# A Fourier layer on one core: norms applied at the images, mixing on two engines, half blocks of y, and pools that stay open

## The chip, the cores and the metric

The kernel runs on one core of a Trainium2 chip. The metric is the device time of one execution in microseconds (us). The time before is the median of three executions. The profile comes from one more execution with the hardware profiler; its clock starts at the start of the profiled span, and all positions below are on that clock. TensorE (PE) does matmuls, VectorE (DVE), ScalarE (ACT) and GpSimd (POOL) work elementwise, and SyncE (SP) only issues DMA transfers. ACT and POOL issue transfers too.

## The reference, cut to what matters

The program is two layers on an image x of 256 x 256 pixels and 128 channels. Layer 0 is an attention along rows with a gate; it ends near 1660 us in the profile and nothing of it changes. Layer 1 regards its input as 256 tokens of 128 x 128 pixels (two halves of 128 tokens, one row of the partitions for each token), attends between tokens in Fourier space, and then runs a block on groups of four tokens. Only this last block is touched:

```python
attn = instance_norm(attn + tokens, ...)         # y in the kernel
h0 = instance_norm(attn, norm2_w, norm2_b)
h1 = fno_layer(h0, mix_wr[0], ..., norm=True, act=True)
h2 = fno_layer(h1, mix_wr[1], ..., norm=True)
out = instance_norm(h2, mon_w, mon_b) + attn

def fno_layer(x, ...):
    skip = einsum('bihw,oi->bohw', x, sw) + sb    # a 4x4 mix of the tokens of a group
    xf = spectral_conv(x, wr, wi, bias)           # 32 x 16 Fourier modes, each a 4x4 complex mix
    if norm: xf = instance_norm(xf)               # mean 0 and variance 1 of each image
    y = xf + skip
    return gelu(y) if act else y
```

The result is added to x. The norm of the spectral part is one factor for each token, called rs: the inverse root of its energy over the modes. So rs times the synthesised image plus the skip product may as well be computed as rs times (image plus skip over rs), if what follows can scale.

## The kernel before, in words

**Tiles.** A half has 128 tokens and 16384 pixels. It is walked in 16 blocks of NB = 2048 pixels, or 32 half blocks of HB = 1024 (512 KB in f32). `by_turn` splits a block into four groups of image columns (j), which belong to the four turned copies that the inverse transform over the height makes from 32 rows of modes each. Half 0's images stay in memory (`blocks`); half 1's y goes to DRAM (`yd`) and comes back.

**Steps of the block.**
- `y_blocks(a, ...)` makes y. For half 1 it writes it with POOL's queue (L1338).
- `first_modes(a)` loads the modes of y, normalises them, mixes them with the 4x4 weights (`mix_modes`), and transforms them over one axis into `Gd1` in DRAM (`synth_modes`, L566 to L589: matmuls, copies out of PSUM by ACT and DVE, writes issued by POOL and ACT).
- `first_images(a)` makes h1 of each block: `skip` (32x32 pieces, L1211) plus `image` (inverse transform of the modes loaded by `load_modes`, L1200), then GELU on ACT (L1499). In the same loop PE transposes the block before and transforms it forward into `Yd`. For half 0 it also computes w = lam y + x on ACT and POOL, and writes it to `wd`.
- `second_modes(a)` reads `Yd` back as YT, finishes the forward transform (L1568), mixes (`mix_modes`), and synthesises into `Gd2`. It also gathers the factors kap and c0 of the last norm.
- `output(a, b)` makes a block of h2 by `skip` and `image`, scales on ACT (L1621), adds w on DVE and writes it out by POOL (L1628). `output_0` runs it for half 0. `Output1` runs it for half 1, and makes w from y and x there (L1674), five half blocks of it ahead.

**Mixing** (`mix_modes`) is 16 products of 128x512 on DVE (L1358), each then added up in PSUM by a matmul with the identity (L1367). After it come the squares on ACT (two, 128x512), the energy by 16 small matmuls (L1376), `rsqrt` (small DVE and ACT operations, L35 to L43), a matmul that spreads the factor over all partitions (L1390), its copy (L1396) and the scaling of both accumulators into Z (L1399). Only then can synthesis begin.

**Order.** The compute engines and SP run in the order in which the program emits work, since the whole block stands under a manual schedule. Stages are generators; the order is made by hand by calling `next` on two of them in turn, at the end of the file. Each engine takes its instructions in order, so a waiting instruction holds all behind it on that engine, SP's loads included.

The stages on the profile's clock are:
- 2047 to 2196: `first_modes(0)` woven with 24 half blocks of `y_blocks(1)`
- 2196 to 2336: `first_images(0)`
- 2336 to 2387: the last 8 half blocks of y and the start of `second_modes(0)`
- 2387 to 2478: `second_modes(0)` and `first_modes(1)`. Both mix, one product each in turn, and then synthesise.
- 2478 to 2680: `first_images(1)` and `output_0` in turn. The pools are changed at the start: `xp` closes with yctx, and `op0` and `hp1` open.
- 2680 to 2755: `second_modes(1)`, with `Output1.ahead` beside its end
- 2755 to 2896: `Output1.run`

The pools are regions of SBUF. A new pool may lie where an old one was, and then its first use waits for the last use of the old. The buffers with names (`xt` 3, `yt` 2, `gs` 3) are taken in turn within a pool, and each waits for the last reader of what it held.

Of the kernel before, what the change touches and what calls it, by code (L numbers as in the profile page):

```python
# [512 lines left out]
def layer1(tc, I, C, ident, x1d, upool, U, stats2, mv2, out):  # L513
# [9 lines left out]
    with ExitStack() as ctx:  # L523
# [681 lines left out]
        def skip(ps, src, blk, stop):  # L1205


            for j in range(4):
                for i in range(4):
                    r, o = slice(32 * i, 32 * i + 32), slice(32 * (i ^ j), 32 * (i ^ j) + 32)  # L1210
                    nc.tensor.matmul(rows_of(ps[j][o, :]), blk[r, r], src[r, j], start=True, stop=stop)  # L1211
# [78 lines left out]
        for a in range(2):  # L1290
            h = Half()
            halves.append(h)
            h.col = sp.tile([P, 16], FP, name=f"col_{a}")
            h.bl0 = sp.tile([P, P], FP, name=f"bl0_{a}")
            h.Gd1 = dram.tile([32, 4, 64, P], FP, name=f"Gd1_{a}")
            h.Gd2 = dram.tile([32, 4, 64, P], FP, name=f"Gd2_{a}")
            h.Yd = dram.tile([H, 32, P], FP, name=f"Yd_{a}")
# [43 lines left out]
        def mix_modes(wp, mk, psum, F, l, tag, out, constant=()):  # L1341
# [3 lines left out]
            T, G = P, P // 4  # L1345
            acc = [psum.tile(f"{tag}acc_{r}") for r in range(2)]
            by_c = [z.rearrange("p (c t) -> p c t", c=4) for z in acc]
# [5 lines left out]
            def product(k):  # L1353
                i, x, r, dst = steps[k]
                t = mk("m", [P, 4, G, 4], f"{tag}m_{k}")
                f = F[:, :, x, :].rearrange("p c (g i) -> p c g i", i=4)[:, :, :, i]
                w = mixw[r][:, :, 16 * l + 4 * i : 16 * l + 4 * i + 4]
                nc.vector.tensor_tensor(t, bc(f, 3, 4), bc(w, 2, G), ALU.mult)  # L1358
                return t.rearrange("p c g o -> p (c g o)")

            t = product(0)
            for k, (i, x, r, dst) in enumerate(steps):
                now = t
                if k < 15:
                    t = product(k + 1)
                yield 0.6
                nc.tensor.matmul(acc[dst], ident, now, start=(i == 0 and x == 0), stop=(i == 3 and x == 1))  # L1367
            sq = mk("f", [P, 2, 4, T], tag + "sq")
            for r in range(2):
                nc.scalar.activation(sq[:, r], by_c[r], AF.Square)  # L1370
            yield 1.8

            en = psum.tile(tag + "ens")
            for c in range(4):
                for r in range(2):
                    nc.tensor.matmul(  # L1376
                        en[:, 0:1], sq[:, r, c, :], om0[:, min(c, 1) : min(c, 1) + 1],
                        start=(c == 0 and r == 0), stop=(c == 3 and r == 1),
                    )
            yield 0.9  # L1380
            rs = wp.tile([P, 2], FP, tag=tag + "rs", name=tag + "rs", bufs=1)
            rsqrt(nc, wp, rs[:, 0:1], en[:, 0:1], EPS, "rq")
            left = rs[:, 1:2]
            nc.vector.tensor_mul(left, rs[:, 0:1], rs[:, 0:1])
            nc.vector.tensor_mul(left, left, en[:, 0:1])
            dg = mk("m", [P, P], tag + "dg")
            nc.vector.tensor_scalar(dg, ident, rs[:, 0:1], None, ALU.mult)
            yield 1.8
            ps = psum.tile(tag + "rsp")
            nc.tensor.matmul(ps[:, 0:T], ones, dg, start=True, stop=True)  # L1390
            for k, (x, m) in enumerate(constant):
                nc.tensor.matmul(
                    ps[0:1, 256 : 256 + T], x, m, start=(k == 0), stop=(k == len(constant) - 1)
                )
            rsb = mk("m", [P, T], tag + "rsb")
            nc.scalar.copy(rsb, ps[:, 0:T])  # L1396
            Z = mk("f", [P, 4, 2, T], tag + "Z")
            for r in range(2):
                nc.vector.tensor_tensor(Z[:, :, r, :], by_c[r], bc(rsb, 1, 4), ALU.mult)  # L1399
            if constant:  # L1400
                nc.vector.tensor_copy(Z[0:1, 0, 0, :], ps[0:1, 256 : 256 + T])
            else:
                nc.vector.memset(Z[0:1, 0, 0, :], 0.0)
            nc.vector.tensor_scalar(Z[0:32, 0], Z[0:32, 0], wsyn[0:32, 0:1], None, ALU.mult)
            out[:] = [Z, left]
            yield 1.8

        def first_modes(a, wp, mk, psum, gts):
# [34 lines left out]
            z = []  # L1443

            yield from mix_modes(wp, mk, psum, F, 0, f"x{a}", z, ((sig, blk[0]), (ch[:, 2:3], ident)))
            Z = z[0]
            for c in range(4):
                synth_modes(wp, psum.pool, Z, P, h.Gd1, f"g1{a}", turned=True, chunk=c, ptag=psum.tag, gts=gts,
                            queues=(nc.gpsimd, nc.scalar))
                yield 2.7  # L1450

        def first_images(a, wp, yp, psk, pst, first=None):
# [5 lines left out]
            def load(b):  # L1458
                if a == 1:
                    ys[b] = yp.tile([P, NB], FP, tag="xt", name=f"y2_{b}")  # L1460
                    nc.sync.dma_start(ys[b], ydv[:, a, b * NB : (b + 1) * NB])
# [27 lines left out]
            for b in range(17):  # L1489
# [4 lines left out]
                if b < 16:  # L1494
                    ps = [psk.tile(f"ups_{a}_{b}_{j}") for j in range(4)]
                    skip(ps, by_turn(ys.pop(b) if a else hb[b]), h.bl0, False)
                    image(ps, gss.pop(b), bs4)
                    for j in range(4):
                        nc.scalar.activation(by_turn(hb[b])[:, j], rows_of(ps[j]), AF.Gelu)  # L1499
# [40 lines left out]
        def second_modes(a, wp, mk, psum, gts, yts):  # L1540
# [6 lines left out]
            def load(c):  # L1547
                yp, tag, bufs = yts[c]
                YT[c] = yp.tile([P, 2, 2, 512], FP, tag=tag, name=f"YT_{a}_{c}", bufs=bufs)
                for hc in range(2):  # L1550
# [7 lines left out]
            load(0)  # L1558
            yield 6.0
            if a:  # L1560
                load(1)
            for c in range(4):
# [12 lines left out]
                for k in ((2,), (3,), (), ())[c] if a else ((1,), (2, 3), (), ())[c]:  # L1575
                    load(k)
                if c < 3:
                    yield 4.0
            yield None
            z = []  # L1580
            yield from mix_modes(wp, mk, psum, F, 1, f"z{a}", z)
            Z, left = z
            Fw = mk("m", [P, 2, P], f"Fw_{a}")
            nc.vector.tensor_scalar(Fw, F[:, 0], hw0, None, ALU.mult)
            for c in range(4):
                if c == 2:

                    ps = psum.tile(f"cvps_{a}")
                    for i in range(4):
                        for r in range(2):  # L1590
                            nc.tensor.matmul(
                                ps[:, 0:P], F[:, i, r, :] if i else Fw[:, r, :], Z[:, i, r, :],
# [4 lines left out]
                    nc.vector.bn_aggr(h.col[:, 10:12], hstat.rearrange("p k s -> p (k s)"))  # L1597
                synth_modes(wp, psum.pool, Z, P, h.Gd2, f"g2{a}", chunk=c, ptag=psum.tag, gts=gts,
                            queues=(nc.gpsimd, nc.scalar))
                yield 2.7  # L1600
# [3 lines left out]
            nc.vector.scalar_tensor_tensor(hv, ps[:, 0:1], 4.0, hv, ALU.mult, ALU.add)  # L1604
            nc.vector.tensor_add(hv, hv, left)
            rsqrt(nc, wp, kap, hv, EPS, "rq")
            nc.vector.tensor_mul(kap, kap, ch[:, 4:5])
            nc.vector.tensor_mul(c0, hm, kap)
# [5 lines left out]
        def output(a, b, gs, w, psk):  # L1614

            kap, c0 = (halves[a].col[:, k : k + 1] for k in (8, 9))
            ps = [psk.tile(f"h2ps_{a}_{b}_{j}") for j in range(4)]
            skip(ps, by_turn(hb[b]), blk[1], False)
            image(ps, gs, bs4)
            for j in range(4):  # L1620
                nc.scalar.activation(  # L1621
                    by_turn(hb[b])[:, j], rows_of(ps[j]), AF.Identity, bias=c0, scale=kap
                )
# [6 lines left out]
        def output_0(pools, psk):  # L1630
# [3 lines left out]
            def load(b):  # L1634
                wp, gp, bufs, _ = pools
                t = wp.tile([P, NB], FP, tag="xt", name=f"w_{b}", bufs=bufs)
                nc.sync.dma_start(t, wd[:, b * NB : (b + 1) * NB])
                gs = gp.tile([P, 4, P], FP, tag="gs", name=f"gs3_0_{b}", bufs=3 if gp is xp else 2)
# [5 lines left out]
            for b in range(16):  # L1644
                if b not in got:
                    load(b)
                if b < 15 and pools[3]:
                    load(b + 1)
                t, gs = got.pop(b)
                yield from output(0, b, gs, [t[:, 0:HB], t[:, HB:]], psk)  # L1650
                yield

        class Output1:
# [23 lines left out]
            def ahead(self):  # L1677
                self.more = self.wp
                self.load(0)
                self.load(1)  # L1680
                yield 1.0
                for k in range(5):
                    self.add(k)
                    if k < 3:
                        self.load(k + 2)
                    yield 1.0

            def run(self, psk, more):
# [11 lines left out]
                for k in (5, 6, 7):  # L1700
# [14 lines left out]
        with tc.manual_schedule(engines=COMPUTE | {ENG.SP}):  # L1715
# [8 lines left out]
            with yctx:  # L1724
# [7 lines left out]
                with tc.tile_pool(name="mp1", bufs=1) as wp:  # L1732
# [10 lines left out]
                    for _ in range(3):  # L1743
                        next(m1)
                    run(iter(lambda: next(m0), None))
                    for _ in m0:
                        next(m1)
                    pools = [xp, xp, 3, True]
                    o0 = output_0(pools, bq)
# [7 lines left out]
                    pools[3] = False  # L1757
                    for _ in range(3):
                        next(o0)
            with tc.tile_pool(name="op0", bufs=4) as op, tc.tile_pool(name="hp1", bufs=2) as wp:  # L1760
                pools[:] = [op, wp, 4, True]
                due, begun = 0.0, False
                for done in first_images(1, wp, op, bq, br, (y2, g2)):
                    if not done:
                        due += 0.9
                        begun = due > 0
                    if begun:
                        next(o0, None)
                    if done and begun:
                        due -= 1.0  # L1770
                run(o0)
            pz.release_now()
            with tc.tile_pool(name="op1", bufs=2) as op:
# [179 lines left out]
```

## Time and profile before

| what | us |
|---|---|
| time, median of 3 | 2890.99 (2890.81 to 2894.68) |
| profiled execution | 2898.24 |
| its span | 2896.1 |
| PE busy | 2640.4 (91%) |
| DVE busy | 2007.2 (69%) |
| POOL busy | 1647.4 (57%) |
| ACT busy | 1463.0 (51%) |

The mean granted clock of PE is 0.948 of full speed. Most of the busy time is layer 0's; the changed part is the last 849 us, so shares of the whole span tell little about it. The rows that matter to it, with their count and mean of one:

| line | operation | count | mean ns |
|---|---|---|---|
| L1358 | DVE product 128x512 | 64 | 684 to 691 |
| L1367 | PE matmul with the identity, 128x512, two passes a product | 128 | 592 |
| L1399 | DVE scaling of Z, 128x512 | 8 | 682 to 686 |
| L1334 | DVE y out of PSUM, 128x256 | 256 | 415 |
| L1499 | ACT GELU 128x512 | 128 | 601 |
| L1621 | ACT scale and bias 128x512 | 128 | 777 |
| L1674 | DVE w = lam y + x, 128x1024 | 32 | 1285 |
| L303 | POOL tensor_tensor 128x512 (layer 0) | 512 | 1270 |
| L327 | POOL tensor_tensor 128x256 (layer 0) | 256 | 732 |
| L299 | POOL tensor_tensor 128x1024 (layer 0) | 256 | 2370 |

The busy time of PE is modelled from pipelined matmuls, and one pass of L1367 follows the next after 0.43 us. DVE's products in a row follow each other after 0.61 us, and those of L1334 after 0.35. The first product of `skip` in each block of `first_images(1)` (tile `ups`) starts at 2487.77, 2511.27, 2523.45, 2532.87, 2544.99 and so on to 2665.68 for the sixteenth.

### The profile page before, as it was taken

Reading aid. Unit: us, or ns where it says so; the run is one execution under the profiler, and the core shown is the slowest. Engines: PE = TensorE matmul, PEld = TensorE weight load, DVE = VectorE, ACT = ScalarE, POOL = GpSimd, SP = SyncE. Lnnn points to the kernel's source line nnn. Section 1 sums busy time; section 2 is a strip of 40 time slices with the busy share of each in tenths; the row PEclk is TensorE's granted clock in tenths of the full one; section 3 lists DMA queues with packets and bytes.
Section 4 is the critical chain, followed back from the end, with each engine's and each line's share of the span. In section 5 each row is a group of like instructions: output and inputs, shape, how many; then the busy total and the mean of one; then the engine's idle time right before and its main releaser. Section 6 shows DMA issues by size and latency. Waiting matters only on the chain. (4 is left out here: it accounts for less than half of the span.)

```text
span 2896.1 us, 70186 instructions
## 1 busy us (share of the span) xinstructions
PE 2640.4 (91%) x28524; PEld 1920.0 (66%) x28524; DVE 2007.2 (69%) x3239; ACT 1463.0 (51%) x2844; POOL 1647.4 (57%) x1282
## 2 busy tenths in 40 slices
PE   6799999999999999999999899999889987688664
PEld 6677777777777777777777656778665565354432
DVE  7788888888888888888888744756655545356445
ACT  0477777777777777777777512200004501354132
POOL 0399999999999999999999700200015721111011
PEclk9999999999999999999999999999999998799865
DMA  9421222222222222222222101188888983897598
GB/s 371 160 71 64 69 68 68 70 65 67 70 67 67 67 67 67 67 67 67 68 68 67 42 16 53 42 275 276 267 295 299 317 304 84 273 362 277 187 351 338
DMA packets 240955, 430.02 MB, mean 148 GB/s; under 512 B 26038, under 2 KB 169865, under 8 KB 232312
## 3 DMA queue, kind: packets, MB, share of 16 engines
q1 hardware_dynamic: 200184, 333.24, 34.8%
q0 software_dynamic: 23552, 83.90, 7.7%
q10 hardware_dynamic: 16896, 8.39, 1.1%
q8 instruction: 226, 3.70, 0.6%
q14 instruction: 97, 0.79, 0.1%
HBM read 290.17 MB, written 135.27 MB: 147 GB/s over the span
## 5 line engine op out<-in xcount | busy, mean ns | idle before, releaser
L299 POOL TENSOR_TENSOR e<-e,b1T 128x1024 f32<-128x1024 f32 x256 | 606.7, 2370 | 163.5 <-PE u L348 89.8
L303 POOL TENSOR_TENSOR es<-e 128x512 f32<-128x512 f32 x512 | 639.5, 1270 | 20.1
L281 ACT ACTIVATE sc<-sc,b2T 128x512 f32<-128x512 f32 x512 | 339.0, 662 | 364.6 <-PE sc L272 356.4
L323 DVE RECIPROCAL av<-av 128x256 f32<-128x256 f32 x256 | 452.3, 1767 | 27.2 <-DVE og L322 1.4
L281 ACT ACTIVATE e<-sc,b2T 128x512 f32<-128x512 f32 x512 | 348.7, 681 | 0.0
L294 DVE TENSOR_TENSOR e<-sc,b1T 128x1024 f32<-128x1024 f32 x256 | 311.0, 1215 | 0.0
L272 PE MATMUL sc<-qkT 32*128 32x256 f32 x4096 | 293.6, 400 | 1.3 <-DVE e L294 1.3
L311 PE MATMUL av<-e,v 128*32 128x256 f32 x4096 | 274.7, 385 | 0.5 <-POOL e L299 0.5
L1324 PE MATMUL yps<-xt,mpT 128*128 128x256 f32 x1024 | 244.9, 393 | 21.1 <-DVE yt L1334 12.7
L272 PEld LDWEIGHTS sc<-qkT 32*128 32x128 f32 x4096 | 185.3, 184 | 112.3 <-issue 97.8
L322 DVE SCALAR_TENSOR_TENSOR og<-gate,av 128x256 f32<-128x256 f32 x256 | 107.7, 421 | 190.6 <-PE av L316 190.6
L1324 PEld LDWEIGHTS yps<-xt,mpT 128*128 128x128 f32 x1024 | 194.5, 195 | 59.1 <-DVE yt L1334 16.3
L1338 POOL DMA_DIRECT2D yd<-yt x32 | 17.4, 545 | 346.5 <-DVE yt L1334 346.5
L327 POOL TENSOR_TENSOR x<-xt,bo 128x256 f32<-128x256 f32 x256 | 187.4, 732 | 0.0
L246 PE MATMUL qk<-xnT,wT_wq 128*128 128x256 f32 x512 | 179.5, 432 | 1.7 <-ACT xnT L238 1.7
L252 PEld LDWEIGHTS gv<-wT_wv,kvT 128*128 128x128 f32 x1024 | 155.0, 192 | 13.4
L316 PE MATMUL av<-es,ones 128*32 128x256 f32 x2048 | 157.5, 379 | 2.6 <-POOL es L303 2.5
L333 PE MATMUL wo<-wT_wo,og 128*128 128x128 f32 x1024 | 156.8, 276 | 2.7 <-DVE og L324 2.7
L1621 ACT ACTIVATE blocks<-h2ps,col 128x512 f32<-128x512 f32 x128 | 89.0, 777 | 138.5 <-PE h2ps L1200 130.2
L311 PEld LDWEIGHTS av<-e,v 128*32 128x32 f32 x4096 | 107.0, 109 | 76.1 <-POOL e L299 1.0
L348 PE MATMUL u<-adft,x 128*128 128x129 f32 x1024 | 156.4, 275 | 0.0
L252 PE MATMUL gv<-wT_wv,kvT 128*128 128x128 f32 x1024 | 156.0, 275 | 0.0
(524 smaller groups left out, 5204.6 us busy)
## 6 DMA issues: line engine op xcount, KB each, us to landing
xt<-x1d SPq DMA_DIRECT2D x128, 512.0 KB
xb<-in_x_dram SPq DMA_DIRECT2D x32, 1024.0 KB
xt<-in_x_dram SPq DMA_DIRECT2D x128, 256.0 KB
kt<-in_L_conv_kv_x_dram SPq DMA_DIRECT2D x128, 256.0 KB
x1d<-x SPq DMA_DIRECT2D x256, 128.0 KB
gs<-Gd SPq DMA_DIRECT2D x384, 64.0 KB
yd<-yt POOLq DMA_DIRECT2D x32, 512.0 KB, 5.7
xw<-x1d SPq DMA_DIRECT2D x32, 512.0 KB
```

The costliest lines, as they stand in the source:

```text
L246: nc.tensor.matmul(ps[:, 0:256], wT["wq"], xnT, start=True, stop=True)
L252: nc.tensor.matmul(ps[:, 256 + c * P : 256 + (c + 1) * P], kvT[:, c * P : (c + 1) * P], wT["wv"], start=True, stop=True,)
L272: nc.tensor.matmul(sc[h // 2][:, h % 2, c * 256 : (c + 1) * 256], qkT[p, 256 + c * P : 256 + (c + 1) * P], qkT[p, 0:256], start=True, stop ...
L281: nc.scalar.activation(r["e"][1][:, :, c, :] if hp else z, z, AF.Exp, bias=b2T[:, c, s : s + 1])
L294: nc.vector.tensor_tensor(r["e"][0].rearrange("p h c q -> p (h c q)"), r.pop("sc").rearrange("p h x -> p (h x)"), b1T[:, 0:2].rearrange("p ...
L299: nc.gpsimd.tensor_tensor(e1, e1, b1T[:, 2:4].rearrange("p h c q -> p (h c q)"), ALU.mult)
L303: nc.gpsimd.tensor_tensor(r["es"][hp], e[:, :, 0, :], e[:, :, 1, :], ALU.add)
L311: nc.tensor.matmul(ps[hd, 0:256], r["v"][:, c, hd], r["e"][h // 2][:, h % 2, c, :], start=(c == 0), stop=(c == 1),)
L316: nc.tensor.matmul(ps[32 * h : 32 * h + 32, 256:512], self.ones, r["es"][h // 2][:, h % 2, :], start=True, stop=True,)
L323: nc.vector.reciprocal(rd, rd)
L327: nc.gpsimd.tensor_tensor(r["x1"], r["x"], bc(self.bo, 1, 2), ALU.add)
L1324: nc.tensor.matmul(rows_of(ps[j]), mpT[:, sc, tt], by_turn(xt[:, sc])[:, j], start=(sc == 0), stop=False,)
```

## The change

- `mix_modes` sends every third product to POOL, can work on two of the four channels at a time (two products then lie in one tile), and ends with the sums in PSUM.
- `mixed` copies the sums into Z without a norm, with ACT and DVE side by side. `norm` computes energy, rs and a row of 1/rs for all partitions. It is called between the chunks of synthesis.
- The skip weights of a half (`bl0`) are multiplied by 1/rs, so that the image plus skip comes out over rs. `first_images` multiplies by rs in the GELU instruction (scale and bias from `h.turn`, in which the factors of the four turned copies stand side by side). `output` does the same through `krs` = kap times rs.
- `second_modes` weaves the last two forward transforms into the first half of the mixing. For half 1 it loads the first halves of YT_0 and YT_1 ahead, and issues the writes of `Gd2` from SP instead of POOL.
- `first_modes(1)` begins later against `second_modes(0)`: it gets a turn on every fourth step of the first part.
- Ahead of half 1's images no pool closes; only `hp1` opens. `w` uses `xp`'s three `xt` buffers. y comes as half blocks, in three buffers (one `wx`, two `yt`), and `skip` takes a list of parts.
- `Output1.ahead` prepares four half blocks instead of five, with ACT and POOL instead of DVE.

The diff, cut to its core:

```diff
 def skip(ps, src, blk, stop):
+    parts = src if isinstance(src, list) else [src]
+    for k, part in enumerate(parts):
+        n = slice(k * 4 // len(parts), (k + 1) * 4 // len(parts))
...
+                w = blk[r, r] if len(blk.shape) == 2 else blk[r, j]
+                nc.tensor.matmul(rows_of(ps[j][o, :])[:, n], w, part[r, j], start=(k == 0), stop=stop)
...
-def mix_modes(wp, mk, psum, F, l, tag, out, constant=()):
+def mix_modes(mk, acc, F, l, tag, cs):
...
+    of = 4 // n
+    def products(k):
+        made = mk("m", [P, 4, G, 4], f"{tag}m_{cs.start}_{k}")
+        for q in range(of):
...
+            (nc.gpsimd if (k + q) % 3 == 2 else nc.vector).tensor_tensor(
+                made[:, q * n : (q + 1) * n], bc(f, 3, 4), bc(w, 2, G), ALU.mult
+            )
...
+def mixed(mk, acc, tag):
+    by_c = [z.rearrange("p (c t) -> p c t", c=4) for z in acc]
+    Z = mk("f", [P, 4, 2, P], tag + "Z")
+    nc.scalar.copy(Z[:, :, 0, :], by_c[0])
+    nc.vector.tensor_copy(Z[:, :, 1, :], by_c[1])
...
-    nc.scalar.activation(by_turn(hb[b])[:, j], rows_of(ps[j]), AF.Gelu)
+    nc.scalar.activation(
+        by_turn(hb[b])[:, j], rows_of(ps[j]), AF.Gelu,
+        bias=h.turn[:, 2 * j + 1 : 2 * j + 2], scale=h.turn[:, 2 * j : 2 * j + 1],
+    )
...
 def load(b):    
     if a == 1:
-        ys[b] = yp.tile([P, NB], FP, tag="xt", name=f"y2_{b}")
-        nc.sync.dma_start(ys[b], ydv[:, a, b * NB : (b + 1) * NB])
+        ys[b] = []
+        for k in (2 * b, 2 * b + 1):
+            pool, tag, bufs = (wp, "wx", 1) if k % 3 == 0 else (yp, "yt", 2)
+            ys[b].append(pool.tile([P, HB], FP, tag=tag, name=f"y2_{k}", bufs=bufs))
+            nc.sync.dma_start(ys[b][-1], ydv[:, a, k * HB : (k + 1) * HB])
...
+    for k, t in enumerate(mix_modes(mk, acc, F, 1, f"z{a}", range(0, 2))):   # second_modes
+        if k in (1, 5):
+            forward(2 + k // 4)
+        yield t
     yield None
+    yield from mix_modes(mk, acc, F, 1, f"z{a}", range(2, 4))
+    Z, sq = mixed(mk, acc, f"z{a}")
...
-            queues=(nc.gpsimd, nc.scalar))
-        yield 2.7
+            queues=(nc.sync if a else nc.gpsimd, nc.scalar))
+        yield 2.4
+        if c == 0:
+            yield next(tail)
+            yield next(tail)
+        if c == 1:
+            run(tail)
...
 def load(b):      # output_0
-    t = wp.tile([P, NB], FP, tag="xt", name=f"w_{b}", bufs=bufs)
+    t = xp.tile([P, NB], FP, tag="xt", name=f"w_{b}", bufs=3)
...
 def ahead(self):  # Output1
+    for half in range(2):
+        for k in (2 * half, 2 * half + 1):
+            self.load(k)
+        yield
+        for k in (2 * half, 2 * half + 1):
+            y = self.ld[k][1]
+            nc.scalar.activation(y, y, AF.Identity, scale=halves[1].col[:, 3:4])
+        yield
+        for k in (2 * half, 2 * half + 1):
+            self.w[k], y = self.ld.pop(k)
+            nc.gpsimd.tensor_tensor(self.w[k], self.w[k], y, ALU.add)
...
 # run
-    for k in (5, 6, 7):
+    for k in range(4, 8):
         self.load(k)
...
-    for _ in range(3):
-        next(m1)
-    run(iter(lambda: next(m0), None))
+    next(m1)
+    for k, _ in enumerate(iter(lambda: next(m0), None)):
+        if k % 4 == 3:
+            next(m1)
...
-with tc.tile_pool(name="op0", bufs=4) as op, tc.tile_pool(name="hp1", bufs=2) as wp:
-    pools[:] = [op, wp, 4, True]
+with tc.tile_pool(name="hp1", bufs=2) as hp:
...
-    for done in first_images(1, wp, op, bq, br, (y2, g2)):
+    for done in first_images(1, hp, xp, bq, br, ([y2[:, 0:HB], y2[:, HB:]], g2)):
```

## The prediction

> **What bounds the kernel now.** The change touches only the second half of layer 1, so I first cut the end of the span into its stages and asked for each one's busy time (columns: PE, weight loads, DVE, ACT, POOL, each with its instructions; then TensorE's granted clock, the DMA share, GB/s).
>
> ```profile
> 2047.00:2196.00 149.00, 131.06 (x1364) 99.28 (x1368) 86.74 (x205) 9.84 (x17) 18.82 (x32) 0.98 0.83 279
> 2196.00:2336.00 140.00, 130.35 (x1883) 68.13 (x1876) 79.35 (x130) 74.12 (x110) 105.55 (x80) 0.99 0.93 317
> 2336.00:2387.00 51.00, 43.20 (x452) 34.29 (x452) 22.63 (x51) 0.59 (x1) 5.05 (x9) 0.90 0.89 302
> 2387.00:2478.00 91.00, 69.98 (x1004) 46.01 (x1004) 49.29 (x119) 13.89 (x29) 11.95 (x16) 0.83 0.43 126
> 2478.00:2512.00 34.00, 19.11 (x200) 8.96 (x208) 4.72 (x4) 10.40 (x16) 2.16 (x4) 0.60 0.76 256
> 2512.00:2680.00 168.00, 146.44 (x2688) 79.07 (x2680) 101.31 (x140) 86.44 (x146) 26.63 (x44) 0.96 0.89 312
> 2680.00:2755.00 75.00, 44.54 (x612) 29.00 (x612) 31.52 (x63) 7.45 (x14) 6.49 (x9) 0.79 0.58 187
> 2755.00:2896.00 141.00, 78.25 (x992) 48.82 (x992) 71.12 (x59) 44.46 (x64) 17.09 (x32) 0.57 0.94 351
> ```
>
> I call the rows B, C, D1, D2, E1, E2, F, G. B, C and E2 are near both PE's and the DMA engines' limit. G is transfers alone. Nothing is full in D2, E1 and F: 200 us of latency. There the chain of waits says what is late. E1 first (start, length, what):
>
> ```profile
> 2465.30 12.16 DMA Gd<-g11gt
> ...
> 2479.03 5.98 DMA gs<-Gd
> ...
> 2487.77 0.62 PE ups L1211
> ...
> 2493.95 2.08 ACT blocks L1499 x4
> 2496.02 0.27 SPq L1461
> ...
> 2500.27 7.68 DMA gs<-Gd
> ...
> 2511.27 3.91 PE ups L1211 x29
> ```
>
> From the landing of half 1's last synthesised modes (2465.30 + 12.16 = 2477.5) to block 1's skip product it takes 33.8 us, though block 0's came at 2487.8. Between them SP stands: its load of y for block 1 (L1461) is issued at 2496.0, since the new pools lie on memory of the old one and wait for w_0 and w_1 to be written out. Then F:
>
> ```profile
> 2679.76 2.72 DMA Yd<-yA
> ...
> 2703.36 2.83 PE f1ps L1568 x48
> 2706.21 0.44 DVE F L1574
> 2706.67 0.70 DVE z1m L1358
> 2707.42 13.45 PE z1acc L1367 x28
> ...
> 2729.22 1.20 DVE z1Z L1399 x2
> ...
> 2731.07 6.69 PE g21gp L566 x128
> ```
>
> Four things in a row: transforms waiting for YT, 15 us of mixing, 8.9 us of norm (2722.2 to 2731.1, with one x add of 1.29 in it), synthesis.
>
> **What the Trainium skill says.** "SBUF — State Buffer", section "Who interferes with whom": a DVE instruction with two SBUF inputs and a GpSimd instruction that reads SBUF exclude each other for the whole instruction. The mixing products are such instructions. The trace of before has no such pair side by side, so it neither confirms nor denies it. "GPSIMD Engine Reference", section "3.1 Elementwise — side-by-side cycle accounting", has a tensor_tensor 1.96 times as long on GpSimd. Here POOL's 128x1024 add (L299) takes 2370 ns and DVE's multiply-add of that size (L1674) 1285: 1.84 times. "DMA: Bandwidth & Descriptors", section "Issuing engines are not separate DMA queues": all queues share the 16 engines, so another issuing engine saves only issue time. G agrees: at a DMA share of 0.94 it doesn't matter who issued.
>
> **The change part by part**, gains in us of the profiled execution (2898.2, span 2896.1; 7.2 above the median 2891.0).
>
> *Sharing the mixing.* Per x mixing, 5 of 16 products (128x512) go to POOL at 1.27 (row L303) and 11 stay on DVE at a cadence of 0.61. With exclusion the sum is 11×0.61 + 5×1.27 = 13.1, without it 6.7 and 6.4 side by side; DVE alone took 16×0.61 = 9.8. PE needs 32 passes of 0.43 = 13.7. So PE hides it either way. For z, 32 products of 128x256: 22×0.35 (row L1334) + 10×0.73 (row L327) = 15.0 with exclusion, against PE's 13.7. I take exclusion: nothing gained in x, 1.3 lost in z. What remains is the order: z may begin with two of its four channels.
>
> *B.* Norm off the path: about 6 earlier to the synthesis, two y blocks sooner. But the synthesis goes through one staging tile, and PE's y blocks fill the stage at 131 of 149 anyway; a POOL product stands behind a yd write (L1338) that waits for yt, so PE's short idle remains. 0, from −4 to +3.
>
> *C.* GELU gets scale and bias: 601 ns (L1499) against 777 for the Identity with both (L1621), so 4×0.18 = 0.7 a block, 11 over 16 blocks, on an ACT busy for 74 of 140 beside a busy PE. −1.5, from −5 (half of the 11 uncovered) to 0.
>
> *D.* z0's mixing ran 2396.3 to 2424.7, interleaved one to one with x1's, and its norm to 2432.2. Now it starts before the last two transforms and x1 lags with 10 of 16 products left. PE: z0 13.7 + 6×0.86 of x1 = 18.9, plus two transforms of about 2; so z0 ends near 2417, synthesis at 2418.5, 13.7 earlier. x1's ten products (8.6) and its synthesis now lie beside z0's synthesis instead of behind it; x1's norm (6) leaves its path. PE has 21 idle of 91 to give. x1's last modes land near 2468, not 2477.5. I take 8: from 2 (x1 pays back its lag) to 14 (all of z0's lead).
>
> *E.* No pool change: y's halves for block 1 and the modes need no out transfer to finish. Block 0's skip product still follows the landing by 10.3 (modes load 6 and its issue); block 1's by 4 to 6 more instead of 23.5, as all it needs is in memory or in flight. Gain at the start 18, less some 5 that the next blocks give back to DMA: 13. Block to block, 2511.27 to 2665.68 over 14 blocks is 11.0; undisturbed stretches run at 10.65; PE alone at 9.4. w's loads no longer displace y's: 14×0.3 = 4. Floor: E moved 34×256 + 168×312 = 61 MB, which at G's 351 to 390 is 157 to 174 us; 202 − 17 = 185 stays above. The skip product becomes 64 passes of half width instead of 32 (L1211, 2.0 a block): the same columns, so 0, at most 1 a block if a narrow pass costs as much as half a wide one more, inside the 1.2 that PE has over in a cycle of 10.65. 17, from 5 to 24.
>
> The price is on SP. y's half-tiles are three, so load(b+1)'s second half waits for PE's first half of skip b, and behind it in SP's order stand that block's modes (4 issues of 0.42), w (0.42) and output modes (4 of 0.42): 4 us of issue and 6 to 8 to land, 10 to 12, against a cycle of 10.65. It fits if block b+1's image needs the modes a cycle and some 2 later.
>
> *F, G.* YT_0 and YT_1's first halves are loaded before the last Yd write; after its landing (te + 2.7, te = 2679.8) the second halves take 6, the two transforms 6.5: te + 15.5. Two MB of y and x stand ahead of YT_2 and YT_3 (5.5 at 365 GB/s), these land by te + 20.5, inside the mixing. Mixing and two woven transforms: 15 + 2×2 = 19: te + 34, not 42.5. Gain 8.5. Raw Z by ACT and DVE side by side, 0.69 plus two small ones: 1.6 instead of 8.9, gain 7.3. Energy and rsqrt (2725 to 2729 in the old order) now run beside the synthesis, and ACT's table for the square root, 1.28 a load elsewhere in the trace (L1499), is loaded before te. Gd writes leave POOL (0.45 issue) for SP: 1. Four pairs instead of five are prepared; G reads 1 MB more: −2.8. Sum 14. POOL's adds of x_0 and x_1 (2×2.37) come before its first products: they may hold the mixing for up to 5. From 8 to 19.
>
> *Sum*: 0 − 1.5 + 8 + 17 + 14 = 37.5. Profiled 2898.2 − 37.5 = 2860.7, median 2891.0 − 37.5 = 2853.5, so 2854. Half-widths 3.5, 2.5, 6, 9.5, 5.5 combine to 13: 2841 to 2868.
>
> **Rivals.**
> *Exclusion bites*: POOL products and adds hold PE, 2 in D, 5 in F: 2861. For it, the skill's rule above; against, POOL has only every third product, and products are made a step ahead of PE.
> *Hidden by the transfers*: E2 and G are at 0.89 to 0.94 of the DMA engines, so D's lead and the steady gain vanish. Left: D 4, E 8, F 8 = 20: 2871.
> *More*: all upper ends of D, E, F with C's cost: 13 + 24 + 18 = 55: 2836. For it, E's floor leaves 28.
> *Slower*: SP's fixed order in E. If the wait for the skip product, the issues and the landing run into the same loop as output modes of the previous block, the cycle is 4 + 8 + about 2 = 14 or more. Without E's steady gain the rest is 8 − 1.5 + 13 + 14 = 33.5; spread over 14 blocks that is 2.4, so it decides from a cycle of 11.0 + 2.4 = 13.4. At 14.3: 46 − 33.5 = 12.7 lost: 2904. For it, SP is in order and the half-tiles are three where whole tiles were four; against, the order of loads is that of their use.
>
> **How the numbers follow.** Forecast 0.35, exclusion 0.10, hidden 0.22, more 0.12, slower 0.18, gains that just cancel 0.03. Faster by over 0.2% (5.8 us; about what this measurement can tell from no change): 0.35 + 0.10 + 0.22 + 0.12 = 0.79. Within: 0.03. Slower: 0.18. Range 2830 to 2894: leaves out the slower case and the lowest part of "more".
>
> **What would show it.** Right: second ups within 17 of the last Gd<-g11gt landing; ups every 10.7; z1acc's end to the first g21gp under 2; g20's first synthesis by 2420 on before's clock; GELU near 0.78 with C no longer than 145; G near 144. Exclusion: POOL products well over 1.27 or 0.73, or DVE's over 0.69. Wrong: a ups cycle over 13 with PE waiting for gs or y behind SP; mixing in F ending after te + 42; x1's last modes landing after 2477.

## The result and the profile after

The changed kernel takes 2890.64 us (median of 20 executions, 2880.80 to 2902.11) against 2891.24 for the kernel before (20 executions, 2881.54 to 2901.05). The ratio on record is 0.9995, with a 95% interval from 0.9982 to 1.0008 (it is not simply the quotient of the two medians, which is 0.9998): no difference that can be measured. The forecast was 2854.

The profiled execution has a span of 2888.9 us, 7.2 less than before's. 2.9 of these were gained before x0's mixing, where both kernels do the same work (first x0acc at 2069.6 and 2072.5). A single pair of profiles is no measurement of the total, but it shows where the time of each stage went. The stages by busy time, as before, with the borders moved to where the stages now begin and end:

```profile
2047.00:2200.00 153.00, 132.62 (x1302) 101.27 (x1300) 83.14 (x195) 9.98 (x17) 23.49 (x35) 0.94 0.77 264
2200.00:2340.00 140.00, 133.22 (x1937) 68.59 (x1932) 82.92 (x135) 85.64 (x110) 105.75 (x80) 0.99 0.93 318
2340.00:2387.00 47.00, 39.73 (x344) 30.72 (x345) 18.26 (x42) 0.59 (x1) 3.98 (x7) 0.82 0.84 281
2387.00:2482.00 95.00, 76.30 (x1106) 55.94 (x1120) 49.65 (x140) 13.59 (x27) 27.19 (x31) 0.84 0.41 130
2482.00:2511.00 29.00, 17.55 (x288) 8.58 (x256) 5.81 (x6) 11.21 (x17) 3.65 (x6) 0.82 0.94 304
2511.00:2680.00 169.00, 156.82 (x3168) 87.81 (x3169) 102.16 (x141) 97.28 (x148) 26.38 (x43) 0.98 0.94 324
2680.00:2722.00 42.00, 28.34 (x336) 21.45 (x340) 18.33 (x31) 7.67 (x9) 17.06 (x15) 0.84 0.52 186
2722.00:2889.00 167.00, 89.56 (x1309) 59.52 (x1303) 84.35 (x100) 49.16 (x74) 18.66 (x33) 0.62 0.91 328
```

B has grown, its DMA share has fallen from 0.83 to 0.77 and PE's clock from 0.98 to 0.94. The start of half 1's images (E1, 29 us instead of 34) is shorter and fuller. To compare without the choice of borders I take the distances between marker instructions from the views by tile and PE's timeline. These are differences of the starts, except where an end is named:

| stage | from, to | before | changed | gain |
|---|---|---|---|---|
| B | first x0acc, first ups of half 0 | 121.5 | 130.4 | −8.9 |
| C | to the last ups of half 0 | 123.9 | 122.4 | 1.5 |
| D | to the last g11gp | 150.2 | 159.1 | −8.9 |
| E1 | to ups of block 1, half 1 | 43.2 | 29.5 | 13.7 |
| E2 | to ups of block 15 | 154.4 | 154.9 | −0.5 |
| F | te (end of the last yA copy), first g21gp | 51.6 | 41.6 | 10.0 |
| G | to the end of the span | 165.0 | 167.4 | −2.4 |

So E1 and F bring 23.7 us, as stages. B, D and G give back 20.2. What E1 brings only makes up for B and D: block 1's skip product starts at 2511.02, and before at 2511.27.

The chain that ended last, in the changed kernel. It goes now through x1, the half that lags:

```profile
2454.39 2.09 PE x1acc L1381 x2
...
2475.01 3.40 PE g11gp L576 x124
...
2479.07 2.75 PE g11gp L576 x124
...
2487.18 7.89 DMA gs<-Gd
...
2498.98 0.62 PE ups L1215
...
2511.02 0.63 PE ups L1215 x8
```

x1's last product is added at 2454.4, while in the kernel before its accumulation ended at 2429.2. Block 1's skip product follows the end of the modes by 29 us instead of 43, and SP no longer stands for the pools.

### The profile page after: what moved, and what is told of

Read it like the earlier page. It is cut to its first block, busy times and chain, and to the rows that moved or that the text cites. A ratio compares the mean times of both kernels' runs of the same rounds, so it can differ in the third digit from the quotient of the medians.

```text
span 2888.9 us, 71477 instructions
## 1 busy us (share of the span) xinstructions
PE 2651.2 (92%) x29116; PEld 1941.7 (67%) x29116; DVE 2008.1 (70%) x3263; ACT 1491.0 (52%) x2849; POOL 1679.9 (58%) x1308
## 5 line engine op out<-in xcount | busy, mean ns | idle before, releaser
L1332 PE MATMUL yps<-xt,mpT 128*128 128x256 f32 x1024 | 247.7, 396 | 17.8 <-DVE yt L1342 9.3
L1346 POOL DMA_DIRECT2D yd<-yt x32 | 17.8, 555 | 346.1 <-DVE yt L1342 346.1
L348 PE MATMUL u<-adft,x 128*128 128x129 f32 x1024 | 156.4, 275 | 0.0
## 6 DMA issues: line engine op xcount, KB each, us to landing
x1d<-x SPq DMA_DIRECT2D x256, 128.0 KB
```

Of the source, the lines that this page charges most:

```text
L1332: nc.tensor.matmul(rows_of(ps[j]), mpT[:, sc, tt], by_turn(xt[:, sc])[:, j], start=(sc == 0), stop=False,)
```

## The experiments

Twelve kernels were run. The table gives the stages of each by the same markers, in us, and the ratio to the kernel before with its interval. The kernel before ran beside each group of runs (its medians lie between 2890.92 and 2893.19), so ratios are what to compare.

| run | B | C | D | E1 | E2 | F | G | median | ratio |
|---|---|---|---|---|---|---|---|---|---|
| e1_all_dve | 127.0 | 123.9 | 157.0 | 30.1 | 155.2 | 41.3 | 167.0 | 2888.94 | 0.9997 (0.9985 to 1.0009) |
| e2_gelu_plain | 130.5 | 125.1 | 156.4 | 28.9 | 152.0 | 39.8 | 169.8 | 2888.38 | 0.9984 (0.9970 to 0.9998) |
| e3_x_norm_first | 121.6 | 123.6 | 156.5 | 29.4 | 152.8 | 41.5 | 169.9 | 2878.93 | 0.9957 (0.9942 to 0.9971) |
| e4_pools_only | 120.2 | 125.1 | 149.4 | 33.5 | 151.1 | 49.2 | 164.1 | 2877.75 | 0.9964 (0.9952 to 0.9975) |
| e5_old_order | 130.5 | 128.4 | 160.0 | 29.3 | 153.6 | 40.1 | 168.7 | 2897.29 | 1.0015 (1.0005 to 1.0025) |
| e6_adds_dve | 126.2 | 125.5 | 156.6 | 29.3 | 152.6 | 42.5 | 167.2 | 2894.38 | 1.0009 (0.9999 to 1.0019) |
| e7_best | 122.1 | 121.3 | 154.8 | 32.2 | 151.8 | 40.4 | 168.6 | 2876.29 | 0.9945 (0.9927 to 0.9963) |
| e8_best_adds | 121.5 | 124.8 | 152.3 | 28.8 | 152.9 | 40.3 | 166.3 | 2874.17 | 0.9937 (0.9916 to 0.9959) |
| e9_z_whole | 128.0 | 123.3 | 152.0 | 28.7 | 156.4 | 40.7 | 168.7 | 2881.83 | 0.9967 (0.9956 to 0.9979) |
| e10_z0_norm_first | 120.6 | 126.9 | 150.0 | 31.0 | 153.8 | 39.8 | 166.7 | 2877.85 | 0.9961 (0.9946 to 0.9976) |
| e11_five_pairs | 121.7 | 125.7 | 151.5 | 34.7 | 154.5 | 39.3 | 169.1 | 2879.56 | 0.9957 (0.9945 to 0.9968) |
| e12_cover | 122.8 | 122.9 | 159.5 | 29.2 | 155.3 | 42.6 | 168.8 | 2886.89 | 0.9982 (0.9971 to 0.9993) |

There is one profile of each kernel, and stages that no edit touched differ: B from 126.2 to 130.5 (changed, e2, e5, e6, e9), C by up to 6, D from 156.4 to 159.5 (changed, e2, e6, e12), E1 from 31.0 to 34.7 (e10, e11), E2 from 152.6 to 156.4, G from 167.0 to 169.9. So a stage's difference of 4 us or less is not read here, and none in C. The profiled executions of e4 and e10 were the fastest of their kernels, so sums of their stages are not the medians.

**All products on DVE.**

```diff
-(nc.gpsimd if (k + q) % 3 == 2 else nc.vector).tensor_tensor(
+nc.vector.tensor_tensor(
```

> The changed kernel, with every mixing product on DVE again. Changed kernel by its trace: first synthesis stretch of half 0 (rhops matmul to the first ups) 140.2 us, first z0acc to end of g11 86.1, te (last yA copy end) to first g21gp 41.3. Theory N (deferring x's norm ate the gains, not the sharing): all three stay within 3 us, time 2886 to 2892. Theory M (POOL and DVE exclude each other, and that made the mixing late): 5, 6 and 4 us shorter, time near 2876.

B is 3.4 shorter, a little more than theory N allows, but e6, in which B is not edited, has 126.2, so this is within what B does by itself. D, F and the time are as expected by theory N. No help and no harm of the sharing can be measured. In the changed kernel's timelines of DVE and POOL (start, length, operation) one sees why it can't help:

```profile
2080.95 1.30 DVE L1368 TENSOR_TENSOR x0m<-F,mixwi 128x512 f32<-128x512 f32 x1
2082.91 0.69 DVE L1368 TENSOR_TENSOR x0m<-F,mixwr 128x512 f32<-128x512 f32 x1 [0.66 <-PE x0acc L1381]
```

```profile
2080.63 1.06 POOL L1368 TENSOR_TENSOR x0m<-F,mixwn 128x512 f32<-128x512 f32 x1
```

POOL's product ends at 2081.69. DVE's, begun at 2080.95, ends 0.56 after that, and takes 1.30 instead of the 0.69 of its neighbour. So it is with each of the five products of x0 that DVE begins beside one of POOL's (1.22 to 1.30): they stood while POOL worked. That is what the Trainium skill states in "SBUF — State Buffer", section "Who interferes with whom", and what the prediction took for granted without having seen it.

**GELU without scale and bias.**

```diff
-by_turn(hb[b])[:, j], rows_of(ps[j]), AF.Gelu,
-bias=h.turn[:, 2 * j + 1 : 2 * j + 2], scale=h.turn[:, 2 * j : 2 * j + 1],
+by_turn(hb[b])[:, j], rows_of(ps[j]), AF.Gelu
```

> The changed kernel, with GELU without scale and bias, so the norm factor and the mean's bias are left out of h1. Undisturbed distance of ups in half 1's images is 10.48 us in the changed kernel, GELU 4 in 2.79. Theory N (the longer GELU holds PSUM banks and so PE): distance 9.4 to 9.9, the images of half 1 about 8 us shorter unless the DMA engines take over, time 2880 to 2885. Theory R (the transfers set that distance): 10.4 or more as now, time 2888 to 2893.

The third shortest distance of two ups, taken as the undisturbed one, is 10.20 instead of 10.48, which neither theory had. E2 is 2.9 shorter, too little to be read, and the time can't be told from the changed kernel's by the intervals; it lies in theory R's range. So theory N's 8 us are not there. What E2 is full of is shown by the windows 2520 to 2660 of the kernel before, the changed one, and this run, in this order:

```profile
2520.00:2660.00 140.00, 123.28 (x2368) 68.24 (x2378) 83.61 (x115) 75.18 (x127) 22.74 (x37) 0.98 0.97 342
```

```profile
2520.00:2660.00 140.00, 129.56 (x2708) 74.41 (x2708) 83.97 (x115) 82.14 (x124) 22.73 (x37) 0.98 0.99 343
```

```profile
2520.00:2660.00 140.00, 125.92 (x2736) 72.93 (x2736) 84.00 (x115) 74.79 (x126) 22.72 (x37) 0.99 1.00 347
```

ACT is busy for 7 us less without scale and bias, PE for 3.6, and yet the DMA share stays at 0.97 to 1.00 and 342 to 347 GB/s in all three. This points to the transfers as what holds E2. It is read from the share: no run took transfers out of the stage. In all fourteen kernels E2 lies between 151 and 157.

**x's norm in front of its synthesis.**

```diff
-Z, sq = mixed(mk, acc, f"x{a}")
-tail = norm(wp, mk, psum, h, sq, f"x{a}")
+# squares, energy, rsqrt, row of rs, Z = sums * row, as before; then the four chunks
...
-bias=h.turn[:, 2 * j + 1 : 2 * j + 2], scale=h.turn[:, 2 * j : 2 * j + 1],
```

This run has e2's plain GELU too, since the norm is applied ahead of it again.

> The changed kernel with x's norm back in front of the synthesis and a plain GELU; z's norm stays deferred, mixing stays shared, pools and half blocks stay. Theory N: stretch rhops to first ups back from 140.2 to about 131, undisturbed ups distance under 10, first z0acc to end of g11 78 to 84 (the lag of x1 stays), time 2868 to 2876. Theory M: rhops to ups stays above 137, time 2885 or more.

B is back at 121.6, D stays at 156.5, and the time falls to 2878.93, a little less than theory N had; the end of g11, 85.7 after the first z0acc, missed its 78 to 84. The plain GELU alone (e2) left B at 130.5. So it is the deferral of x's norm that costs B its 4 to 9 us: the kernels with it have 126.2 to 130.5, those without 120.2 to 122.1. Only e12, which puts y blocks into the gaps of the deferral, lies between.

**Only the pools and half blocks.** The edit puts the changed `skip`, `output_0`, the loads of y and the order ahead of half 1's images into the kernel before.

> The kernel before with only the part on pools and half blocks of y (no pool change ahead of half 1's images, w in xp's buffers, skip in two parts). In before: end of g11 to ups of block 1 is 42.9 us, block 1 to block 15 154.4. Theory N: 29 to 31 and 147 to 154, time 2874 to 2879. Theory R (the transfers only move: what the start gains is given back over the blocks): 29 to 31 and 163 to 168, time 2887 to 2892.

E1 falls by 9.7 (to 33.5; 29 to 31 were expected), E2 isn't longer, and the time, 2877.75, is in theory N's range. This part of the change alone is a gain of 0.36% (0.25 to 0.48), more than all parts together have. Theory R, by which the transfers would take it back, falls.

**The old order of half 1's first modes.**

```diff
-next(m1)
-for k, _ in enumerate(iter(lambda: next(m0), None)):
-    if k % 4 == 3:
-        next(m1)
+for _ in range(3):
+    next(m1)
+run(iter(lambda: next(m0), None))
```

> The changed kernel, with half 1's first_modes given its turns as before: three ahead of z0, then one for each step of z0's second half (x1 does not lag). From the last ups of half 0 to the end of g11: before 150.2 us, changed 159.1. Theory N (x1's lag by ten products costs this): 149 to 153, time 2881 to 2886. Rival Q (the products of half width and the norm between the chunks cost it): 156 or more, time 2888 to 2893.

D is 160.0, as rival Q had it, and the time 2897.29, worse than either expected. x1's mixing still ends 56.6 after the first z0acc (59.8 in the changed kernel, 32.4 before). The edit was not the old order in effect. z0 is mixed two products to a step, so its second half has only 8 steps, and x1 gets 8 turns beside it instead of 16. Hence e9.

**The adds on DVE.**

```diff
-nc.scalar.activation(y, y, AF.Identity, scale=halves[1].col[:, 3:4])
-nc.gpsimd.tensor_tensor(self.w[k], self.w[k], y, ALU.add)
+self.add(k)     # one DVE multiply-add of 128x1024
```

> The changed kernel, with the four adds ahead of the last output as DVE multiply-adds of 1.29 us again instead of ACT scale and POOL add. Changed kernel: from te to the first g21gp 41.6 us, of which DVE's products stood 5.07 (two that take 0.8) and its scaling of F 2.43 beside POOL's adds. Theory L (POOL's adds lock DVE out, and that is on the path): 36 to 39, time 3 to 6 less, 2885 to 2888. Rival (YT's landing sets it, and DVE's own 5.2 take its place): 41 to 43, time within 2.

F is 42.5, and the rival is right on it: the first z1acc comes 19.4 after te instead of 15.0, since DVE's own adds now stand ahead of its products, and the mixing ends within 1 us of where it did. The time can't be told from the changed kernel's. In the changed kernel the exclusion is there all the same. These are two DVE products and POOL's adds in F:

```profile
2695.15 5.07 DVE L1368 TENSOR_TENSOR z1m<-F,mixwr 128x256 f32<-128x256 f32 x2
```

```profile
2694.84 5.09 POOL L1767 TENSOR_TENSOR x<-x,y 128x1024 f32<-128x1024 f32 x2 [13.90 <-DMA x<-x1d]
```

It cost PE nothing there. DVE's two products were done by 2700.22, and PE's next instructions were the third transform, which waited for YT_2, and only then more mixing:

```profile
2698.32 0.64 PE L1610 MATMUL f1ps<-YT,k_efwd 128*32 128x128 f32 x16 [2.24 <-DMA YT<-Yd]
2699.67 2.65 PE L1610 MATMUL f1ps<-YT,k_efwd 128*32 128x128 f32 x48 [0.71 <-DMA YT<-Yd]
2702.25 4.61 PE L1381 MATMUL z1acc<-z1m,ident 128*128 128x256 f32 x16
```

**z0 mixed in one piece, with the old order.**

```diff
+if a:
+    ...             # half 1 as in the changed kernel
+else:
+    forward(2)
+    yield 4.0
+    forward(3)
+    yield None
+    yield from mix_modes(mk, acc, F, 1, f"z{a}", range(4))
```

> The changed kernel with the old order and z0 mixed in one piece (128x512 products) after all four transforms; x's norm stays deferred, sharing stays. Theory N (the halves of z give x1 only half as many turns, and that is its lag): end of x1's mixing 33 to 37 after the first z0acc, first z0acc to end of g11 72 to 76 instead of 85.9, last ups of half 0 to first z0acc 77 to 82, time 2884 to 2889. Rival (the deferred norm between x1's chunks keeps g11 late): end of g11 still 82 or more after the first z0acc, time 2889 to 2894.

The view by tile of x1's matmuls, changed kernel and then this run (shortest, median, longest in ns; first and last start):

```profile
L1381 PE MATMUL x1acc<-x1m,ident x32: 592/592/1222, 2416.7 to 2455.4; 128*128 128x512 f32 x32
```

```profile
L1381 PE MATMUL x1acc<-x1m,ident x32: 592/592/697, 2401.9 to 2431.0; 128*128 128x512 f32 x32
```

x1's mixing ends 24 us earlier and takes 29.1 us instead of 38.7; its end is 34.9 after the first z0acc, as theory N had it. From the first z0acc to the last g11gp it is 71.7 instead of 86.0. D as a whole is 152.0, since the two transforms now lie ahead of z0acc. The time, 2881.83, is below theory N's range. The edit takes the halves, the woven transforms and the lag away together, so the lag's part is not measured alone; e5, which had the halves and kept most of the lag, kept the loss. B stays at 128.0 with x's norm deferred. So B and D are two separate losses.

**Both undone.** e7_best has e3, e9 and all products on DVE; e8_best_adds has DVE's adds as well.

> The changed kernel with x's norm in front of the synthesis, plain GELU, the old order, all products on DVE, and z0 mixed in one piece after all four transforms as before; from the change remain the pools, half blocks, z's deferred norm, and all of half 1's last part. Theory N, by stages against before: B 0, D -2 to -4, start of half 1's images -13, F -10, last output +2 to +5: 2864 to 2872. Rival (the transfers take back what is earlier): 2875 to 2880, as with the pools alone.

> As the run with the label e7_best, and the four adds on DVE. Theory L: from te to g21gp 36 to 39, 2 to 4 less than e7_best. Rival: within 1.5 of e7_best.

2876.29 and 2874.17: 0.55 and 0.63% under the kernel before. e7 is slower than theory N had it and lies in the rival's range (2875 to 2880). By stages it isn't the transfers that took the rest, E2 being 151.8, but D, at 154.8 where 146 to 148 were expected. F differs by 0.1 between the two, so theory L falls here too.

**z0's norm in front, and five pairs.** e10 also puts z0's norm back ahead of its synthesis; e11 prepares a fifth half block on top of that (`self.load(4)`, `self.add(4)` at the end of `ahead`).

> As the run with the label e8_best_adds, and z0's norm too in front of its synthesis, so that only half 1's z has a deferred norm. Theory N (in half 0 x1's path sets the end, so an earlier z0 gains nothing): from the last ups of half 0 to the end of g11 148 to 151 instead of 152.3, time 2868 to 2874. Rival (deferring z0's norm did gain): 155 or more, time 2878.

> As e10_z0_norm_first, and a fifth half block prepared ahead of the last output, as before. First g21gp to the end: 166 to 168 with four. Theory T (the last stage is transfers, 1 MB at 351 to 390 GB/s): 2.5 to 3 shorter, 163 to 165. Rival (the fifth load and add stand ahead of the modes' writes and loads): 166 or more.

D is 150.0, as theory N had it, but from 152.3 this is within the spread, and the time isn't shorter: 2877.85. With five pairs G is 169.1, not 163 to 165, and theory T falls. None of e7, e8, e10 and e11 can be told from another by their intervals. e10 is nearly e4 with the new F, and has the same median: the 9.4 that F is shorter do not show in the total. Where they go stays open. The profiles have E2 and G longer by 2.7 and 2.6, which is within what such stages vary by, and the two intervals leave room for a gain of some us.

**Cover for x0's norm.**

```diff
 Z, sq = mixed(mk, acc, f"x{a}")
-yield 1.2
+yield 3.0
...
+    yield 1.8     # twice, between the parts of the norm's tail
```

> The changed kernel, and in half 0's first modes blocks of y put in between: one between the end of x0's mixing and its first synthesis, two between the parts of the norm's tail (the weights, the bias, the turned copies). From first x0acc to first ups of half 0: before 121.5, changed 130.4 (126.2 to 130.5 in the runs so far that defer x's norm, 120.2 to 122.1 in those that don't). Theory W (the deferral took away the y blocks that had covered PE's waits for DVE and ACT, and PE's clock falls after each wait): 122 to 125, time 2883 to 2888. Rival (the added matmuls and DVE work of the turned factors cost it): 127 or more, time 2888 to 2894.

B is 122.8 with all of the deferred norm's work in it, so the work is not what costs. (One wait of 2.94 is left in its norm's tail.) B and the time, 2886.89 (0.18% under the kernel before), are as theory W had them, though the time's interval overlaps the changed kernel's. PE's timeline in the changed kernel and in e12:

```profile
2117.07 3.72 PE L576 MATMUL g10gp<-x0Z,k_esyn 32*64 32x128 f32 x128 [2.94 <-ACT x0sq L1397]
2120.72 4.84 PE L1332 MATMUL yps<-xt,mpT 128*128 128x256 f32 x16
...
2153.08 0.38 PE L1474 MATMUL x0rsp<-col,blk 128*128 128x1 f32 x2 [2.58 <-DVE bl L1471]
```

```profile
2114.68 3.62 PE L1332 MATMUL yps<-xt,mpT 128*128 128x256 f32 x16
2118.23 0.73 PE L1200 MATMUL yps<-bsy,gs 32*128 32x128 f32 x16
2118.89 2.09 PE L576 MATMUL g10gp<-x0Z,k_esyn 32*64 32x128 f32 x128
2120.91 3.72 PE L1332 MATMUL yps<-xt,mpT 128*128 128x256 f32 x16
```

In the changed kernel PE waits 2.94 us for raw Z, and then the synthesis takes 3.72 and the y block 4.84, while with a y block in the gap they take 2.09 and 3.72. In this kernel the wait of 2.94 costs 2.94 + 1.63 + 1.12 = 5.7. That is not a fixed price. In e6 the same wait had no slow matmuls behind it:

```profile
2119.07 2.08 PE L576 MATMUL g10gp<-x0Z,k_esyn 32*64 32x128 f32 x128 [2.94 <-ACT x0sq L1397]
2121.08 3.72 PE L1332 MATMUL yps<-xt,mpT 128*128 128x256 f32 x16
```

This is most of why B differs between kernels with the same code there. PE is idle for 17.5 to 17.8 us of B in the changed kernel, e2, e5, e6 and e9, and busy for 112.9, 113.0, 113.0, 108.7 and 110.2.

## Why the prediction was wrong, point by point

- **B, "0".** It measured −8.9. The failing step is "Norm off the path: about 6 earlier to the synthesis". It was earlier (47.5 after the first x0acc, not 59.7), but the norm had not been on a path here: y blocks had filled its waits (one wait of PE over 2 us stood in before's B, 4.86 for yt). In their place came an uncovered wait for Z of 2.94, another of 2.58 in the norm's tail, and slower matmuls. From the first x0acc to the first ups PE is busy for 112.9 instead of 106.8 and idle for 17.6 instead of 14.8: of the 8.9, 2.8 are waits and 6.1 slower or added matmuls. e3 and e12 both take the loss away.
- **C, −1.5.** Nothing can be read: C varies by more between unedited runs.
- **D, "I take 8".** It measured −8.9. Two steps failed. "z0 ends near 2417", 7.7 earlier: counted from the last ups of half 0, z0's mixing begins 5.2 earlier than in the kernel before, but takes 31.2 from first to last start instead of 28.0, so it ends 2.0 earlier, and its synthesis begins 8.1 earlier and not 13.7. The step summed PE's work, 18.9 and about 2. PE was idle for 4.0 of z0's 31.6 us, most of it in front of x1's steps, which stand between z0's in PE's order:

```profile
2411.05 0.67 PE L1449 MATMUL rhops<-dg,ones 128*128 128x256 f32 x2 [1.32 <-DVE dg L1445]
2416.71 2.05 PE L1381 MATMUL x1acc<-x1m,ident 128*128 128x512 f32 x2 [2.36 <-DVE x1m L1368]
```

  The two transforms took 2.86 and 1.95, and the granted clock of this stretch was 0.88. The other step is "x1's ten products and its synthesis now lie beside z0's synthesis". They do, but at one product per step of z0's chunks, so x1's mixing ended 59.8 after the first z0acc instead of 32.4. The step counted PE's idle time and not how often x1 gets a turn. The lowest case of D, "2 (x1 pays back its lag)", left no room for a loss. e9 takes 7 of this loss away, but not to a gain: D was 150.2 before, 152.0 in e9, and 150.0 in e10, where no norm of half 0 is deferred. No run found the 8. In every kernel without the lag the last g11gp comes 71.7 to 74.6 after the first z0acc (71.9 before); what holds it there stays open.
- **E, 17.** The start was right: 13 forecast, 13.7 measured (8.5 to 14.5 in the kernels with the new pools). The 4 of steady gain was not there. The step "14×0.3 = 4" took the undisturbed pace of 10.65 as one that all blocks can keep when w's loads no longer displace y's. But the steady part of E2 was at 0.97 of the DMA engines already in the kernel before, at 342 GB/s and not at G's 351 to 390. The prediction's own rival "hidden by the transfers" named this for E2.
- **F and G, 14.** It measured 10.0 − 2.4 = 7.6. The raw Z was right: the first g21gp came 1.8 after the start of z1's last matmul (8.9 before), so 7.1 of the forecast 7.3. The first z1acc at te + 15.0 was right too (15.5). The step that failed is "Mixing and two woven transforms: 15 + 2×2 = 19: te + 34": from first to last start it took 24.8, to te + 39.8. The third transform stands in PE's order behind the first four passes of mixing, and the last of YT_2 came in at te + 19.8. The prediction has this landing (te + 20.5) and calls it inside the mixing, but its sum runs through the wait. The rival "exclusion, 5 in F" had the right number for another cause: POOL's adds did hold DVE for 5.07, under PE's wait for YT_2, and without them (e6) the mixing ends no earlier. The halves of z1 cost nothing: in e8 and e10, with all of POOL's work in F on DVE, the same halves and transforms take 19.8 and 19.9, but begin at te + 18.8 and 18.1, behind DVE's adds. There a pass of half width takes 0.22, half of 0.43 (e8):

```profile
2692.69 9.76 PE L1381 MATMUL z1acc<-z1m,ident 128*128 128x256 f32 x44
```

  G is longer by about what was forecast for its extra megabyte (2.4 and 2.8), but this is within the spread, and e11, which reads that megabyte ahead, has 169.1: the cause is not shown. Nor is the 1 us for the writes that leave POOL, since no run changed only who issues them.
- **SP's fixed order.** It did not decide. The waits of SP for the skip product are there (engine and line that waited, what for, us in total, times, longest):

```profile
SPq L1503 <- PE ups L1215: 24.6, 10, 6.7
```

24.6 us in 10 waits in the window 2520 to 2660, yet PE waited for y only once there, 1.8 us, and the ups distances are as before.

Added up by stages, −8.9 + 1.5 − 8.9 + 13.7 − 0.5 + 10.0 − 2.4 = 4.5 in the profiles and 0.6 in the medians. The mechanisms of E1 and of the raw Z in F were right. B was put at 0 and D at a gain of 8, and each lost 8.9. That the time still lies within the range stated, 2830 to 2894, is luck: losses that were not foreseen happen to be as large as the gains that were. The case "gains that just cancel" had a chance of 0.03. Of the signs of being wrong one came true: the last writes of x1's modes were issued only at 2483.6 and 2484.3, and so landed after 2477.

## What to carry to other kernels

Work that is off the critical path because something else covers it gains nothing by being moved; look first at what ran in its waits, and what runs there afterwards. When two streams are issued in turns, changing the step of one changes the pace of the other: count turns, not only busy time. When a step is put between others, its wait comes along, so a sum of durations needs the landing times beside it. And before a steady pace is expected to fall, look at the DMA share of just that stretch.

## What the runs showed of the hardware that was not expected

- After the same wait of 2.94 us ahead of half 0's first synthesis, PE's granted clock over the next 9 us was 0.67 in the changed kernel, 0.66 in e2 and e5, 0.81 in e9, 0.84 in e1, and 1.00 in e6. The Trainium skill has the mechanism, a clock gate that follows how busy PE has lately been, in "TensorE: Matmul & The Clock Gate", section "What's actually happening", with a window of about 3.4 us; here a shorter wait was enough in five of six kernels, and in the sixth it was not.
- DVE's scaling of F, 128x256 with one SBUF input, took 2.43 us in F beside POOL's adds, and 0.335 in half 0 and 0.34 in e8, where no POOL add is beside it. So it's not only instructions with two SBUF inputs that stand; "SBUF — State Buffer", section "Who interferes with whom", names this operation among those that can, and the prediction had not drawn on that.
- POOL's 128x512 product of x0 took 1.06 us where layer 0's product of that size takes 1.27, and its 128x256 product 0.61 at the shortest.
